# An LSTM with residual on one core: the input product x·Wx by blocks of 4 steps, replaced by blocks of 24 steps with 20 outer and 7 inner products of 256 columns

## The chip, the core and the metric

The kernel runs on one core of a Trainium2 chip. The metric is the time on the device in microseconds (us), from one launch. Before the change, three runs took 3149.18, 3149.30 and 3149.34 us, so the median is 3149.3 us. The trace comes from one profiled execution.

## The reference, cut to what matters

The input `x` has 32 sequences of 512 steps of 512 values. An LSTM with 512 units runs over the 512 steps, from the state `cond_1024`, and its hidden states are added to `x`. Everything is in float32.

```python
xW = jnp.einsum('ntd,dg->ntg', x, Wx) + b        # all steps: 512 x 2048 weights
def step(carry, xw_t):
    prev_h, prev_c = carry
    a = xw_t + prev_h @ Wh                        # 32 x 512 times 512 x 2048
    i, f, o = sigmoid(a[:, :H]), sigmoid(a[:, H:2*H]), sigmoid(a[:, 2*H:3*H])
    g = jnp.tanh(a[:, 3*H:])
    next_c = f * prev_c + i * g
    next_h = o * jnp.tanh(next_c)
    return (next_h, next_c), next_h
x = x + swapaxes(hs, 0, 1)
```

The recurrent product `prev_h @ Wh` can only be made step by step. The input product `x Wx` is known for all steps from the start, so a kernel is free to make it in any order and by any bilinear scheme.

## The kernel before, in words

**Layout.** A step's 32 sequences are 32 columns of the stationary operand. Four such matmuls, one per quarter `j` of the gates' columns, write to the four 32-row quarters of one PSUM bank and run side by side in the array, so that the gates of a step fill a bank of 128 x 512 numbers.

**A step.** `h_part` (L584) makes the recurrent product: 16 matmuls of 512 columns for one step, accumulated on a bank that already holds the step's input part and bias. `cell` (L614 to L651) is the chain that leads to the next step: three activations on ScalarE, the products `fc`, `ig` and the sum `c` on VectorE, the tanh of `c` (L630), the product `h` (L633) and two 32x32 block transposes to `ht` (L642), on which the next `h_part` waits. GpSimd adds `x` to `ht` for the output (L648), and SyncE stores two steps at a time (L651).

**The input part.** While the chain of `cell` runs, TensorE has to be given other work: the input product of later steps. It is made for four steps at a time (a "quad") by two nested schemes of 7 products in place of 8: `operand` and `inner` (L380) make 7 x 7 products of 4 matmuls with 128 columns each. The sums of weights that the scheme needs lie in SBUF for the whole run (`w_sb`, made at the start by L253 and L258), the sums of `x` are made on VectorE per 8 steps (`early_sums`, `late_sums`, L127 to L171), and the products are put together on VectorE and ScalarE from PSUM (`read_out`, `first_add`, `second_add`, `seed`, L313 to L372, L510 to L519) straight into the banks of the gates. Nothing of it leaves the core.

**Order.** The program order is written by hand: a loop over windows `k` (one per step, after a head) emits `h_part`, the evacuations, the sums of `x`, the input products (`input_part`) and `cell`, and each engine runs its own instructions in that order. The recurrent product of step `t` comes before the input products of the window on TensorE's queue, and `cell` comes behind the evacuations and the sums on VectorE's and ScalarE's queues. The first quads and the last four steps are made with plain products (`direct`, L411).

Of the kernel before, what the change touches and what calls it, by code (L numbers as in the profile page):

```python
# [9 lines left out]
PSUM = bass.MemoryType.PSUM  # L10

# [5 lines left out]
TC = 8  # L17
NCHUNK = T // TC

FIRST = 2  # L20
LAST = T // 4 - 1

SPLIT = 4 * LAST - 2

LEAD = 11
BEGIN = {1: 0, 5: 1, 6: 3, 7: 6, 2: 7, 3: 7, 4: 9}
WINDOWS = T + LEAD

TAIL = T - 19

H = P // 2
# [3 lines left out]
def kernel(  # L35
# [8 lines left out]
):  # L44

    nc = tc.nc

    const = ctx.enter_context(tc.tile_pool(name="const", bufs=1))
    xpool = ctx.enter_context(tc.tile_pool(name="xpool", bufs=3))  # L80
    spool = ctx.enter_context(tc.tile_pool(name="spool", bufs=2))
    upool = ctx.enter_context(tc.tile_pool(name="upool", bufs=1))
    opool = ctx.enter_context(tc.tile_pool(name="opool", bufs=2))
    work = ctx.enter_context(tc.tile_pool(name="work", bufs=1))
    psum = ctx.enter_context(tc.tile_pool(name="psum", bufs=1, space=PSUM))


    pa = [psum.tile([P, 4, P], F32, name=f"pa_{i}") for i in range(3)]
    slot = {1: (0, 0), 7: (0, 1), 5: (1, 0), 4: (1, 1), 6: (2, 0), 2: (2, 1), 3: (2, 2)}
    pb = psum.tile([P, 4, P], F32, name="pb")  # L90
    pbslot = {1: 0, 7: 0, 5: 0, 4: 1, 6: 0, 2: 1, 3: 2}
    pp = psum.tile([P, 4, P], F32, name="pp")
    ge = psum.tile([P, G, P], F32, name="ge")
    go = [psum.tile([P, G, P], F32, name=f"go_{i}") for i in range(2)]

    split_banks = [(ge, pp), (go[1], ge), (pa[1], pa[0]), (pa[2], pb), (go[0], pp), (ge, go[1])]

    def is_split(t):
        return t == 0 or t >= SPLIT

    def bank_of(t, h):

        return (ge, pa[2])[h] if t == 0 else split_banks[t - SPLIT][h]

    def half_of(t, h):

        return bank_of(t, h)[:, 0:2]

    def gates_of(t):
        return ge if t % 2 == 0 else go[(t % 4) // 2]  # L110


    xcs, sums = {}, {}

    def load_chunk(c):
        xc = xpool.tile([P, TC, NJ, B], F32, name=f"xc_{c}", tag="xc")
        nc.sync.dma_start(out=xc.rearrange("p t q b -> p (t q b)"), in_=x[c])
        xcs[c] = xc

    def blocks(c):  # L120

        return xcs[c].rearrange("p (d r s) (k e) b -> p d r s k e b", d=2, r=2, s=2, k=2, e=2)

    def pair_sums(eng, dst, a11, a12, a21, a22):

        return [
            lambda: eng.tensor_add(dst[0], a21, a22),  # L127
            lambda: eng.tensor_sub(dst[1], dst[0], a11),
            lambda: eng.tensor_sub(dst[2], a11, a21),
            lambda: eng.tensor_sub(dst[3], a12, dst[1]),  # L130
        ]

    def inner_sums(eng, dst, a11, a12, a21, a22):
        return pair_sums(eng, [dst[:, i] for i in range(4)], a11, a12, a21, a22)

    def early_sums(eng, c, ds=(0, 1)):

        if c not in sums:
            s = spool.tile([P, 2, 2, 2, 2, B], F32, name=f"sa_{c}", tag="sa")
            n = spool.tile([P, 4, 4, B], F32, name=f"na_{c}", tag="na")  # L140
            n1 = spool.tile([P, 4, 2, B], F32, name=f"n1_{c}", tag="n1")
            sums[c] = {"sa": s, "na": n, "n1": n1}
        v, s, n, n1 = blocks(c), sums[c]["sa"], sums[c]["na"], sums[c]["n1"]
        z = s.rearrange("p i d s e b -> p (i d) s e b")
        if len(ds) == 1:
            d = slice(ds[0], ds[0] + 1)
            v, s, n1 = v[:, d], s[:, :, d], n1[:, :, d]
            n, z = n[:, :, ds[0] :: 2], z[:, ds[0] :: 2]
        f = s.rearrange("p i d s e b -> p i d s (e b)")
        w = v.rearrange("p d r s k e b -> p d r s k (e b)")  # L150
        return [
            *inner_sums(eng, n1, *(v[:, :, 0, i, 0, e] for i in range(2) for e in range(2))),
            lambda: eng.tensor_add(f[:, 0], w[:, :, 1, :, 0], w[:, :, 1, :, 1]),
            lambda: eng.tensor_sub(f[:, 1], f[:, 0], w[:, :, 0, :, 0]),
            *inner_sums(eng, n, *(z[:, :, i, e] for i in range(2) for e in range(2))),
        ]

    def late_sums(eng, c):

        v = blocks(c)  # L160
        s = spool.tile([P, 2, 2, 2, 2, B], F32, name=f"sb_{c}", tag="sb")
        n = spool.tile([P, 4, 4, B], F32, name=f"nb_{c}", tag="nb")
        n2 = spool.tile([P, 4, 2, 2, B], F32, name=f"n2_{c}", tag="n2")
        sums[c] |= {"sb": s, "nb": n, "n2": n2}
        f = s.rearrange("p i d s e b -> p i d s (e b)")
        fa = sums[c]["sa"].rearrange("p i d s e b -> p i d s (e b)")
        w = v.rearrange("p d r s k e b -> p d r s k (e b)")
        z = s.rearrange("p i d s e b -> p (i d) s e b")
        return [
            lambda: eng.tensor_sub(f[:, 0], w[:, :, 0, :, 0], w[:, :, 1, :, 0]),  # L170
            lambda: eng.tensor_sub(f[:, 1], w[:, :, 0, :, 1], fa[:, 1]),  # L171
            *inner_sums(eng, n, *(z[:, :, i, e] for i in range(2) for e in range(2))),
            *inner_sums(eng, n2, *(v[:, :, :, i, 1, e] for i in range(2) for e in range(2))),
        ]

    INNER = {1: (0, 0), 2: (0, 1), 4: (1, 1)}
    SUM = {5: 0, 6: 1, 7: 2, 3: 3}

    def operand(r, s, quad):

        c, d = divmod(quad, 2)
        z = sums[c]
        if r in INNER:
            big, k = INNER[r]
            if s in INNER:
                i, e = INNER[s]
                return blocks(c)[:, d, big, i, k, e]
            return z["n1"][:, SUM[s], d] if r == 1 else z["n2"][:, SUM[s], d, big]
        group = "a" if r in (5, 6) else "b"
        i = {5: 0, 6: 1, 7: 0, 3: 1}[r]  # L190
        if s in INNER:
            return z["s" + group][:, i, d, INNER[s][0], INNER[s][1]]
        return z["n" + group][:, SUM[s], 2 * i + d]

    bias_sb = const.tile([P, G, P], F32, name="bias_sb")
    h_init = const.tile([P, NJ, B], F32, name="h_init")
    w_sb = {r: const.tile([P, 8 if r == 1 else 7, NJ, P], F32, name=f"w_{r}") for r in range(1, 8)}
    w12 = const.tile([P, 4, NJ, P], F32, name="w12")  # L200
    raw = {(0, 0): w_sb[1], (0, 1): w12, (1, 0): w_sb[2], (1, 1): w_sb[3]}

    wh_sb = const.tile([P, NJ - 1, NJ, G * P], F32, name="wh_sb")
    wh_3 = const.tile([P, 2, NJ, G * H], F32, name="wh_3")

    def wh_of(k, j, i=None):

        halves = slice(0, 2) if i is None else slice(i, i + 1)
        if k == NJ - 1:
            return wh_3[:, halves, j]  # L210
        return wh_sb[:, k, j].rearrange("p (i c) -> p i c", i=2)[:, halves]

    def load_raw(k, gg):
        nc.sync.dma_start(
            out=raw[k, gg][:, 0:4].rearrange("p s j u -> p (s j u)"),
            in_=wx[2 * k + gg],
        )

    def load_steps(a, b, c=0):

        if c not in xcs:
            xcs[c] = xpool.tile([P, TC, NJ, B], F32, name=f"xc_{c}", tag="xc")
        nc.sync.dma_start(
            out=xcs[c][:, a:b].rearrange("p t q b -> p (t q b)"),
            in_=x[c][:, a * P : b * P],
        )


    bias_t = const.tile([P, G * NJ], F32, name="bias_t")
# [3 lines left out]
    load_steps(0, 4)  # L233
    load_raw(0, 0)
    load_raw(0, 1)
    load_steps(0, 4, 1)
    load_raw(1, 0)
    load_raw(1, 1)
    load_steps(4, 5)
    nc.sync.dma_start(out=h_init.rearrange("p q b -> p (q b)"), in_=h0)  # L240
    for k in range(NJ - 1):
        nc.sync.dma_start(out=wh_sb[:, k].rearrange("p j c -> p (j c)"), in_=wh[:, k])
    for i in range(2):
        nc.sync.dma_start(
            out=wh_3[:, i].rearrange("p j c -> p (j c)"),
            in_=wh[:, NJ - 1, i * NJ * G * H : (i + 1) * NJ * G * H],
        )
    load_steps(4, 8, 1)
    load_steps(5, 8)

    def outer_weight(r):
# [71 lines left out]
    def slot_of(r, quad):  # L323

        if r == 6 and quad == FIRST:
            return (1, 2)
# [546 lines left out]
```

## Time and profile before

| | |
|---|---|
| median of 3 runs | 3149.3 us |
| span of the profiled execution | 3147.8 us (the median run is 1.5 us longer than it) |
| TensorE busy | 3140.9 us, 100% of the span, granted clock 1.000 |
| VectorE busy | 2263.4 us, 72% |
| ScalarE busy | 1288.8 us, 41% |
| GpSimd busy | 232.8 us, 7% |
| moved by DMA | 86.23 MB, mean 27 GB/s |

The page of the profile gives the busy time of each engine (PE is TensorE's matmuls, DVE is VectorE, ACT is ScalarE, POOL is GpSimd, SP is SyncE). The timeline gives instructions in order of time: start, duration, engine, line, operation, output and inputs, shape, and how many were merged into the row. A float32 matmul stands as two instructions, so that "x8" is four matmuls. Starts of back-to-back rows show the pace of an engine better than durations, since instructions are pipelined and overlap.

### The profile page before, as it was taken

What the parts mean: (1) busy time and instruction counts of PE and PEld (TensorE: products, weight loads), DVE (VectorE), ACT (ScalarE), POOL (GpSimd) and SP (SyncE); (2) the same over time, 40 slices, a digit from 0 to 9 for tenths busy, and PEclk for the clock granted to TensorE, in tenths of its full rate; (3) what the DMA queues carried; (4) which work ended last, traced back from release to release, by engine and by line L of the source; (5) the groups of instructions that cost most, each with busy time, mean ns of one, the idle gap of its engine ahead of it and who ended that gap; (6) DMA issues with size and microseconds to landing.
All of it is one profiled execution on the core that took longest, in us unless ns stands there. A gap on an engine that the chain in (4) does not pass through costs nothing.

```text
span 3147.8 us, 150115 instructions
## 1 busy us (share of the span) xinstructions
PE 3140.9 (100%) x66384; PEld 1901.1 (60%) x66384; DVE 2263.4 (72%) x9338; ACT 1288.8 (41%) x4274; POOL 232.8 (7%) x505
## 2 busy tenths in 40 slices
PE   9999999999999999999999999999999999999999
PEld 5666666666666666666666666666666666666665
DVE  8777777777777777777777777777777777777775
ACT  3444444444444444444344444444344444444343
POOL 1000000000000000000000000000000000000000
PEclk9999999999999999999999999999999999999999
DMA  3000000000000000000000000000000000000000
GB/s 137 26 26 21 26 28 20 28 20 27 27 20 28 20 28 26 21 26 20 28 26 21 26 27 21 28 20 26 28 20 28 20 28 27 21 27 20 28 20 29
DMA packets 49325, 86.23 MB, mean 27 GB/s; under 512 B 5792, under 2 KB 38944, under 8 KB 47776
## 3 DMA queue, kind: packets, MB, share of 16 engines
q1 hardware_dynamic: 48528, 76.63, 7.6%
q8 instruction: 518, 8.49, 1.1%
q14 instruction: 135, 1.11, 0.1%
q10 hardware_dynamic: 144, 0.01, 0.0%
HBM read 43.07 MB, written 33.55 MB: 24 GB/s over the span
## 4 chain that ended last, share of the span: by engine, by line
PE 100%; DMA 0%; DVE 0%; ACT 0%; issue 0%; SPq 0%
PE go L584 28%; PE ge L584 28%; PE pa L380 18%; PE pp L380 10%; PE pb L380 6%; PE ge L380 5%; PE go L380 3%; PE go L411 1%; PE pa L584 0%; PE pp L411 0%; PE pa L411 0%; DMA w<-in_L_cond_Wx_dram 0%; PE pa L438 0%; PE pp L584 0%; PE ge L411 0%; PE ge L438 0%
## 5 line engine op out<-in xcount | busy, mean ns | idle before, releaser
L584 PE MATMUL go<-wh_sb,ht 128*32 128x512 f32 (+1 forms) x6144 | 702.8, 590 | 0.0
L584 PE MATMUL ge<-wh_sb,ht 128*32 128x512 f32 (+1 forms) x6120 | 700.0, 590 | 0.0
L618 DVE TENSOR_TENSOR fc<-s,c 128x128 f32<-128x128 f32 x489 | 143.0, 292 | 496.1 <-ACT s L614 496.1
L614 ACT ACTIVATE s<-ge 128x256 f32<-128x256 f32 (+1 forms) x263 | 99.5, 378 | 829.1 <-PE ge L584 825.5
L648 POOL TENSOR_TENSOR oc<-xc,ht 128x128 f32<-128x128 f32 x493 | 228.1, 463 | 2806.6 <-issue 1404.0
L584 PEld LDWEIGHTS ge<-wh_sb,ht 128*32 128x32 f32 x6120 | 192.8, 110 | 304.8 <-issue 264.4
L584 PEld LDWEIGHTS go<-wh_sb,ht 128*32 128x32 f32 x6144 | 190.9, 110 | 307.0 <-issue 301.3
L380 PE MATMUL pa<-w,n 128*32 128x128 f32 x6000 | 301.1, 273 | 0.0
L630 ACT ACTIVATE ig<-c 128x64 f32<-128x64 f32 x1024 | 208.4, 248 | 222.5 <-DVE c L628 208.8
L614 ACT ACTIVATE s<-go 128x256 f32<-128x256 f32 (+1 forms) x265 | 100.0, 377 | 431.8 <-PE go L584 431.8
L584 PE MATMUL go<-wh,ht 128*32 128x512 f32 (+1 forms) x2048 | 265.2, 590 | 0.0
L584 PE MATMUL ge<-wh,ht 128*32 128x512 f32 (+1 forms) x2040 | 264.2, 590 | 0.0
L633 DVE TENSOR_TENSOR fc<-s,ig 128x64 f32<-128x64 f32 x1024 | 191.0, 225 | 96.0 <-ACT ig L630 96.0
L380 PEld LDWEIGHTS pa<-w,n 128*32 128x32 f32 x6000 | 182.0, 110 | 77.5 <-issue 39.5
L380 PEld LDWEIGHTS pa<-w,na 128*32 128x32 f32 x4000 | 124.6, 110 | 149.5 <-issue 109.9
L318 ACT COPY u<-pp 128x512 f32<-128x512 f32 x250 | 146.6, 586 | 142.4 <-PE pp L380 142.3
L380 PE MATMUL pa<-w,na 128*32 128x128 f32 x4000 | 200.7, 273 | 0.0
L380 PE MATMUL pp<-w,sa 128*32 128x128 f32 x4000 | 200.7, 273 | 0.0
L380 PE MATMUL pa<-w,nb 128*32 128x128 f32 x4000 | 200.7, 273 | 0.0
L642 DVE STREAM_TRANSPOSE ht<-fc 128x64 f32<-128x64 f32 x978 | 182.2, 224 | 1.5 <-DVE fc L633 1.0
L623 DVE TENSOR_TENSOR ig<-s 128x64 f32<-128x64 f32 x1024 | 183.1, 218 | 0.0
L628 DVE TENSOR_TENSOR c<-fc,ig 128x64 f32<-128x64 f32 x978 | 172.9, 218 | 0.0
(195 smaller groups left out, 5686.5 us busy)
## 6 DMA issues: line engine op xcount, KB each, us to landing
out_dram<-oc SPq DMA_DIRECT2D x255, 128.0 KB, 1.8
xc<-in_x_dram SPq DMA_DIRECT2D x62, 512.0 KB, 3.9
w<-in_L_cond_Wx_dram SPq DMA_DIRECT2D x4, 1024.0 KB, 8.6
wh_sb<-in_L_cond_Wh_dram SPq DMA_DIRECT2D x3, 1024.0 KB, 15.2
wh<-in_L_cond_Wh_dram SPq DMA_DIRECT2D x2, 512.0 KB, 15.0
w<-in_L_cond_Wx_dram SPq DMA_DIRECT2D x2, 512.0 KB, 5.2
xc<-in_x_dram SPq DMA_DIRECT2D x3, 256.0 KB, 7.7
xc<-in_x_dram SPq DMA_DIRECT2D x1, 192.0 KB, 11.4
```

The lines of the kernel that those rows point to most:

```text
L318: nc.scalar.copy(u, pp)
L380: nc.tensor.matmul(dst[j * B : (j + 1) * B], operand(r, s, quad), w_sb[r][:, place(r, s), j], start=start, stop=True, skip_group_check=True,)
L411: nc.tensor.matmul(half_of(t, gg)[j * B : (j + 1) * B] if is_split(t) else bank[j * B : (j + 1) * B, 2 * gg : 2 * gg + 2], xcs[c][:, tt, 2 ...
L584: nc.tensor.matmul(g[j * B : (j + 1) * B], state["ht"][:, k, :], wh_of(k, j, i), start=False, stop=True, skip_group_check=True,)
L614: nc.scalar.activation(s[:, i, 0:2], g[:, :, 0:2], AF.Sigmoid)
L618: nc.vector.tensor_mul(by_half(fc), s[:, :, 1], by_half(state["c"]))
L623: nc.vector.tensor_mul(ig[:, u], s[:, i, 0], s[:, i, 3])
L628: nc.vector.tensor_add(c[:, HALVES[i]], fc[:, HALVES[i]], ig[:, HALVES[i]])
L630: nc.scalar.activation(tc_t[:, HALVES[i]], c[:, HALVES[i]], AF.Tanh)
L633: nc.vector.tensor_mul(h[:, u], s[:, i, 2], tc_t[:, u])
L642: nc.vector.transpose(ht[:, 2 * i : 2 * i + 2].rearrange("p q b -> p (q b)"), h[:, HALVES[i]])
L648: (nc.gpsimd if t < TAIL else nc.vector).tensor_add(state["oc"][:, tt % 2], xcs[n][:, tt], ht)
```

## The change

The input product of steps 32 to 511 is made in 20 blocks of 24 steps (3 rows of 8 steps). Each block is a bilinear scheme of 20 outer products over 3x2 by 2x4 blocks, given as tables (`A_OPS`: 13 sums of x blocks, `B_OF`: which blocks of Wx are summed per product, `C_OPS`: 25 sums of products, `C_OF`: the 12 results). Each outer product is made by 7 inner products of 4 matmuls with 256 columns. One outer product is begun per window, five in six windows (`begin`).

- **Weights.** 14 of the 20 products need a sum of blocks of Wx. These sums are made on VectorE in the steps 0 to 9 (`make_factors`), stored to DRAM (`kept`) and loaded again for every block of 24 steps (`fetch`: 384 KB and 512 KB per product).
- **x.** The 13 sums of x blocks (`node_sums`) and four inner sums per product (`inner_sums`) are made on VectorE, in `prepare`, emitted behind `cell` of the window before.
- **Products.** `evacuate` copies and adds the inner products (ScalarE L297, L301, L307, L308; VectorE L304, L309), and `finish_product` makes the sums of `C_OPS` on VectorE, in halves of 512 columns, in 7 SBUF slots.
- **Results.** A finished result, 8 steps by a quarter of the gates, is written to DRAM in four DMAs, so that it lies by step (`store`). Per step, `load_xw` loads 256 KB back three steps ahead, GpSimd adds the bias (`add_bias`, L418, 128 x 512), and ScalarE copies the sum into the bank of the gates (`seed_gates`, L437).
- **Head and tail.** Steps 0 to 7 are plain products (`direct`), steps 8 to 31 are 12 units of 2 x 7 inner products (`finish_unit`). The last product ends in step 494 or before; from step 495 on a step is split into two halves of the units.
- `h_part` and `cell` are as before in their instructions, but the split form is used only in the tail.

The diff is nearly the whole kernel; its core is the new functions:

```diff
+    def make_factors(n):
+        wa, wb = ring(n, f"make_{n}")
+        (first, s0), *rest = B_OF[n]
...
+    def inner_sums(a, name):
+        s = spool.tile([P, 4, 4, B], F32, name=f"s_{name}", tag="sums")
...
+            lambda: v.tensor_add(s[:, 0], a(1, 0), a(1, 1)),
+            lambda: v.tensor_sub(s[:, 1], s[:, 0], a(0, 0)),
+            lambda: v.tensor_sub(s[:, 2], a(0, 0), a(1, 0)),
+            lambda: v.tensor_sub(s[:, 3], a(0, 1), s[:, 1]),
...
+    def products(v):
+        for late, ss in ((1, (6,)), (4, (4,)), (2, (7,)), (0, (1,)), (0, (5,)), (1, (5,)), (3, (2, 3))):
+            job = jobs.get(v - late)
+            for s in ss if job else ():
+                if s != 5 or job.w5 == v:
+                    product(job, s)
...
+    def evacuate(v):
+        for half, late in ((1, 5), (0, 4)):
+            job = jobs.get(v - late)
+            if job:
+                job.finish(half)
...
+        job = jobs.get(v - 2)
+        if job:
+            nc.vector.tensor_add(job.pu[:, 1], job.acc, job.p5)
+        job = jobs.get(v - 3)
+        if job:
+            nc.scalar.copy(job.pp[0], job.pu)
+            nc.scalar.copy(job.pp[1][:, 0], job.acc)
+            nc.vector.tensor_add(job.pp[1][:, 1], job.acc, job.p5)
...
+        def finish(half):
+            pp = job.pp[half].rearrange("p n c -> p (n c)")
+            if n in copied:
+                nc.scalar.copy(slot(n, half), pp)
...
+            for v in by_ready[n]:
+                how, a, b = C_OPS[v - R]
+                fn = nc.vector.tensor_add if how == "add" else nc.vector.tensor_sub
+                srcs = source(a), source(b)
+                fn(slot(v, half), *srcs)
...
+    def load_xw(t):
+        xw[t] = upool.tile([P, 2, C], F32, name=f"xw_{t}", tag="xw", bufs=4)
+        i, a = divmod(t, ROW)
+        nc.sync.dma_start(out=xw[t].rearrange("p n c -> p (n c)"), in_=stored[i][a])
+
+    def add_bias(t):
+        nc.gpsimd.tensor_add(xw[t], xw[t], bias_sb)
...
+        for k in range(T):
+            if k % 2 == 0 and k + 2 < T:
+                load_residual(k + 2)
+            if 2 * 4 - 3 <= k and k + 3 < T:
+                load_xw(k + 3)
+            h_part(k)
+            if 1 <= k < T - 1:
+                seed_gates(k + 1)
+            if 2 * 4 - 2 <= k and k + 2 < T:
+                add_bias(k + 2)
+            for m, v in enumerate(windows_of(k)):
...
+                evacuate(v)
+                products(v)
+                fetch(v)
...
+                if m == 0:
+                    cell(k)
+                    for _ in range(make_at.get(k, 1 if k < START else 0)):
+                        if to_make:
+                            for op in make_factors(to_make.pop(0)):
+                                op()
+                for op in prepare(v + 1):
+                    op()
+                if m == 0 and k < 3:
+                    direct(k + 5, gates[k % 2])
+                    keep_direct(k + 5, gates[k % 2])
```

More of the change, by code (lines that the diff above doesn't have):

```diff
@@ L214, in load_raw, with load_row @@
+    raw = [const.tile([P, 4, C], F32, name=f"raw_{i}") for i in range(8)]
+    tt_ = [const.tile([P, 4, C], F32, name=f"t_{i}") for i in range(8)]
+    single = {b[0][0] for b in B_OF if len(b) == 1}
+    rows, xw, stored = {}, {}, {}
+    def load_row(i, a=0, b=ROW):
+        if i not in rows:
+            rows[i] = xpool.tile([P, ROW, NJ, B], F32, name=f"row_{i}", tag="row")
         nc.sync.dma_start(
-            out=raw[k, gg][:, 0:4].rearrange("p s j u -> p (s j u)"),
-            in_=wx[2 * k + gg],
-        )
@@ new lines, with store @@
+    free = []
+    spare = [const.tile([P, 2, 2 * C], F32, name=f"slot_{i}") for i in range(3)]
+    free += spare
+    others = [t for i in range(8) if i not in single for t in (raw[i], tt_[i])]
+    def store(i, j, f):
+        if i not in stored:
+            stored[i] = dram.tile([ROW, P, 2 * C], F32, name=f"xw_{i}", tag="xw", bufs=6)
+        to = stored[i].rearrange("(g t) p c -> t p g c", g=2)
+        for t in range(4):
+            nc.sync.dma_start(out=to[t, j * B : (j + 1) * B], in_=f[t * B : (t + 1) * B])
@@ new lines, in finish_unit @@
+    def finish_unit(job, i, j):
+        def finish(half):
+            if half == 0:
+                job.f = free.pop(0)
+            nc.scalar.copy(job.f[:, half], job.pp[half].rearrange("p n c -> p (n c)"))
+            if half:
+                store(i, j, job.f)
+                free.append(job.f)
+        return finish
+    ready = list(range(R))
+    for _, a, b in C_OPS:
+        ready.append(max(ready[a], ready[b]))
+    by_ready = {n: [R + i for i in range(len(C_OPS)) if ready[R + i] == n] for n in range(R)}
@@ L743 @@
+    to_make = [n for n in range(R) if len(B_OF[n]) > 1]
+    make_at = {0: 2, 1: 2, 2: 2, 3: 2}
     with tc.manual_schedule():
@@ new lines @@
+        for m in range(10):
+            nc.tensor.matmul(
+                pps[0][0:B].rearrange("p n c -> p (n c)"),
+                c_init[:, 0:B],
+                c_init.unsqueeze(1).to_broadcast([P, 4, P]),
+                start=True,
+                stop=True,
+            )
+        nc.vector.transpose(
+            bias_sb.rearrange("p n (m l) -> p (n m) l", l=B),
+            bias_t.unsqueeze(2).to_broadcast([P, G * NJ, B]),
+        )
+        firsts = [gates[0], gates[1], pps[0], pps[1]]
```

885 lines of the change are left out of this document (327 added, 558 removed).

## The prediction

> **What bounds the kernel now.** I read the page first (busy time and the chain that ended last), then two stretches of windows, then the timeline of one step.
>
> ```profile
> span 3147.8 us, 150115 instructions
> PE 3140.9 (100%) x66384; PEld 1901.1 (60%) x66384; DVE 2263.4 (72%) x9338; ACT 1288.8 (41%) x4274; POOL 232.8 (7%) x505
> ...
> PE 100%; DMA 0%; DVE 0%; ACT 0%; issue 0%; SPq 0%
> ```
>
> ```profile
> 600.00:746.88 146.88, 146.88 (x3136) 89.25 (x3132) 105.44 (x438) 60.46 (x199) 11.03 (x24) 1.00 0.08 24
> ...
> 6.00:16.20 10.20, 9.59 (x188) 7.17 (x192) 8.95 (x21) 0.60 (x2) 0.00 (x0) 1.00 1.00 388
> ```
>
> TensorE never stops, at a granted clock of 1.00; 24 steps take 146.88 us, in which VectorE is busy 105.44. One step, from its first recurrent matmul to the next one:
>
> ```profile
> 1500.62 2.76 PE L584 MATMUL go<-wh_sb,ht 128*32 128x512 f32 x24
> ...
> 1504.06 0.40 PE L380 MATMUL pa<-w,nb 128*32 128x128 f32 x8
> ...
> 1504.31 0.39 ACT L614 ACTIVATE s<-go 128x256 f32<-128x256 f32 x1 [1.33 <-PE go L584]
> ...
> 1504.72 0.29 DVE L618 TENSOR_TENSOR fc<-s,c 128x128 f32<-128x128 f32 x1 [1.28 <-ACT s L614]
> ...
> 1506.07 0.37 DVE L642 STREAM_TRANSPOSE ht<-fc 128x64 f32<-128x64 f32 x2
> ...
> 1506.52 0.46 POOL L648 TENSOR_TENSOR oc<-xc,ht 128x128 f32<-128x128 f32 x1 [5.76 <-DVE ht L642]
> ...
> 1506.68 2.76 PE L584 MATMUL ge<-wh_sb,ht 128*32 128x512 f32 x24
> ```
>
> The recurrent product takes 1504.06 - 1500.62 = 3.44 us. The 12 input products behind it take 2.62 us, so 0.218 each. Beside them runs the chain: `fc` starts 0.66 us after the recurrent product, the transposes end at 1506.44, which is 1.72 after `fc`. The next recurrent matmuls need only the first half of `ht`, some 0.15 earlier; with 0.06 for the hand-over they could start 1.63 after `fc`, so 2.29 us after the recurrent product. That the input products last longer than 2.29 us is what hides the chain. This is the number to watch.
>
> **The change part by part.**
>
> *TensorE, gain.* The new products have 256 columns. Products of that width stand at the start:
>
> ```profile
> 6.61 1.07 PE L411 MATMUL go<-w,xc 128*32 128x256 f32 x16 [1.43 <-DMA w<-in_L_cond_Wx_dram]
> 7.47 1.07 PE L411 MATMUL ge<-w,xc 128*32 128x256 f32 x16
> ```
>
> Two groups of four in 0.86-0.865, so 0.4315 us per product. A block of 24 steps has 20 x 7 = 140 products: 60.4 us, and 24 x 3.44 = 82.6 of recurrent product, 143.0 together against 146.88. All of TensorE's work: 512 x 3.44 = 1761.3; 20 x 60.4 = 1208.2; 12 units x 14 x 0.4315 = 72.5; 8 plain steps of 3.44 = 27.5; in all 3069.5. With the same start at 6.6 and the 4.5 us from the last recurrent matmul (row below, 3142.80 + 0.43 to 3147.8), the time without any stall would be 3080.6, 67 us less than now. The rest of the sum is stalls.
>
> *Tail, loss 21.9 us.* The last products thin out: the steps 490 to 494 have 4, 3, 1, 0 and 0 products against the 2.29 us that the chain needs: stalls of 0.56, 1.0, 1.86, 2.29 and 2.29, together 8.0. From 495 on there are none, but a step is split in halves. The pace of split steps stands at the end of the trace:
>
> ```profile
> 3135.40 1.05 PE L584 MATMUL go<-wh_sb,ht 128*32 128x256 f32 x16
> ...
> 3137.59 1.05 PE L584 MATMUL pp<-wh_sb,ht 128*32 128x256 f32 x16
> ...
> 3139.42 0.24 DVE L635 STREAM_TRANSPOSE ht<-fc 128x64 f32<-128x64 f32 x1
> ...
> 3142.80 0.61 PE L584 MATMUL go<-wh,ht 128*32 128x256 f32 x8
> ```
>
> The first half is ready 2.19 us into a step (from 3135.40 to 3137.59), its transpose ends at 3139.66; with 0.05 the next step starts after 4.31, 0.87 more than its work. 16 times 0.87 is 13.9.
>
> *Head, loss 18.5 us.* VectorE makes the weight sums here, and its queue is in order.
>
> ```profile
> L513 DVE TENSOR_TENSOR p<-u,p 128x512 f32<-128x512 f32 x125 | 86.5, 692 | 114.7 <-ACT u L318 114.7
> L372 DVE TENSOR_TENSOR go<-pa,u 128x512 f32<-128x512 f32 x125 | 85.9, 687 | 0.0
> ...
> L253 DVE TENSOR_TENSOR w<-w,w 128x2048 f32<-128x2048 f32 x4 | 9.1, 2285 | 0.5 <-DMA w<-in_L_cond_Wx_dram 0.5
> ```
>
> From 512 to 2048 columns 1.04 ns each, so 768 columns take 0.95. An addition of `make_factors` (256 and 768 columns) is then some 1.3 to 1.37 us and the four closing ones 1.43. In step 0 VectorE has, behind the chain (2.4 after the recurrent product), two sets of factors with 1 and 3 additions (8.2), the sums for the next unit (2.7), a 512-column and a 256-column addition (1.0): 14.3. TensorE needs the last of them for inner product 7 of unit 0, after 2.6 + 3.44 + 0.86 = 6.9. It waits 7.4. The same sum gives 1.9 in step 1, 3.3 ahead of step 0 (unit 0's sums come behind the keep of step 4) and 5.9 in the steps 2 to 12. By the Trainium skill, TensorE: Matmul & The Clock Gate, section "What's actually happening", an idle window of about 3.4 us halves TensorE's clock until it has been busy for as long again. An estimate by that page is some 2 us more at step 0; no idle time of that length behind the start is in this trace, whose clock is 1.00 throughout.
>
> So without the steady part: 3080.6 + 21.9 + 18.5 = 3121.
>
> *Steady part: VectorE's queue.* VectorE's evacuations and sums of x stand on its queue ahead of `fc` of the next step, and it is on VectorE that the change adds: 13 x-block sums, 80 inner sums, 50 halves of C_OPS, 40 additions of 256 columns per 24 steps.
>
> ```profile
> 1506.54 0.41 DVE L342 TENSOR_TENSOR xr<-pb,bias_sb 128x256 f32<-128x256 f32 x1
> ...
> 1506.87 0.41 DVE L367 TENSOR_TENSOR u<-pa,u 128x256 f32<-128x256 f32 x1
> ```
>
> ```profile
> 3100.16 0.69 DVE L372 TENSOR_TENSOR go<-pa,u 128x512 f32<-128x512 f32 x1
> 3100.76 0.42 DVE L486 TENSOR_TENSOR pa<-pa,bias_sb 128x256 f32<-128x256 f32 x1
> ```
>
> ```profile
> 42.92 0.46 POOL L648 TENSOR_TENSOR oc<-xc,ht 128x128 f32<-128x128 f32 x1 [5.80 <-DVE ht L635]
> 43.34 1.28 POOL L258 TENSOR_TENSOR w<-w 128x512 f32<-128x512 f32 x1
> ```
>
> ```profile
> 43.47 0.42 DVE L356 TENSOR_TENSOR pp<-pa,u 128x256 f32<-128x256 f32 x1
> 43.80 0.97 DVE L127 TENSOR_TENSOR n<-xc 128x128 f32<-128x128 f32 x1
> 44.80 0.29 DVE L128 TENSOR_TENSOR n<-n,xc 128x128 f32<-128x128 f32 x1
> 45.01 0.28 DVE L129 TENSOR_TENSOR n<-xc 128x128 f32<-128x128 f32 x1
> 45.22 0.29 DVE L130 TENSOR_TENSOR n<-xc,n 128x128 f32<-128x128 f32 x1
> 45.42 0.69 DVE L258 TENSOR_TENSOR w<-w 128x512 f32<-128x512 f32 x1
> ```
>
> Start to start: 256 columns 0.33, 512 columns 0.60 (0.72 where the next reads its result), four inner sums 0.94 (0.32 for the dependent one, then 0.2 each). The price per window: an x-block sum 0.72, inner sums 0.94, each C_OPS half 0.6 or 0.72, `pu` and `pp` 0.33 each. The budget: with six products (2.59) the transposes end 0.21 before the next recurrent matmuls start, and VectorE begins its next op some 0.07 earlier, as ops overlap at their ends; `fc` is due 3.44 + 0.66 = 4.10 after. So 4.38 us of other work fit, 4.68 before TensorE stalls (six products last 2.59, 0.30 more than 2.29). After a window that stalled, the transposes end later against the matmuls and the bounds are 4.08 and 4.38. Every sixth window has five products, 2.16 us, and stalls 0.13 in any case.
>
> By the tables, window 0 of a block has one x-block sum, four inner sums, four C_OPS halves, `pu` and `pp`: 0.72 + 0.94 + 2.5 + 0.66 = 4.8, or 5.0 with ScalarE's copy between (L308 waits for the C_OPS, L309 for L308); window 7 has 4.5, 18 4.4, 23 4.0, all others under 3.8. That alone stalls 0.4 in window 0 and 4 x 0.13: 0.93 per block, 18.6 in all.
>
> *What comes on top: GpSimd.* It gets a 128 x 512 addition per step (L418), right behind the addition for the output, at the time when VectorE begins with the sums of x. The rows above show what that does: the 128-column sum L127, 0.29 elsewhere, took 0.97 because it came while GpSimd's 128 x 512 op ran (43.34 to 44.62), and ended 0.15 behind it; L356, which reads PSUM, was not touched (0.42). So a VectorE op with both inputs in SBUF is held until the GpSimd op is over. In the changed kernel GpSimd runs from 0.15 to about 1.9 us after VectorE becomes free. The inner sums and x-block sums fall into this time: where they would be over after 0.94, they are over after some 2.2, 1.1 to 1.3 us later; in windows without sums, a C_OPS of two SBUF sums is held for 1.0. With the full hold, VectorE's work in windows 0 to 23 is 6.1, 4.2, 3.7, 4.0, 3.0, 1.4, 4.7, 5.7, 3.8, 3.4, 4.9, 3.7, 4.8, 4.7, 3.7, 4.6, 4.9, 3.7, 5.5, 4.9, 4.4, 4.2, 4.9, 5.0. Against the bounds, the stalls are 1.8 (window 0), 1.36 (7), 0.90 (18), 0.65 (23), 0.49 (15, 20), 0.44 (19), five of 0.19 to 0.25, and the rest: 7.7 per block, 154 in all. With three quarters of the hold the same sum gives 4.2 and 84, with half 2.4 and 48, with a quarter 1.4 and 28. The lower bound is no hold (18.6), as VectorE might get ahead between two GpSimd ops; the upper one the full hold. The nearest row is the full one, but a single row with one long op does not show who goes first when both wait. I take the middle between three quarters and full: 119.
>
> *Hidden.* The bias is added and loaded two to three steps ahead. ScalarE has at most 2.9 us of copies per window against some 4.3. The weights come two windows ahead of their use. Per block DMA moves 12.5 MB of weights, 6.3 out and 6.3 back of results, 4.7 of x and output: 30 MB in some 148 us, 200 GB/s, where the second row of windows has 388 GB/s at a DMA share of 1.00. That is cover of nearly two; the DMA issues stay hidden behind it.
>
> Sum: 3121 + 119 = 3240 of span, 1.5 more as a median: **3242 us**, 2.9% slower.
>
> **The rivals.**
>
> - *VectorE is not held* (the other side). If VectorE's sums go ahead of GpSimd's addition, or the addition comes later, while VectorE works on PSUM: 3121 + 18.6 + 1.5 = 3141, 0.26% faster. For it: nothing in the trace shows the two waiting for one another again and again. Against: the one row that has the pair. The point where it decides is a quarter of the hold, 28 us, where the time is 3150.
> - *Half the hold*: 3121 + 48 + 1.5 = 3171.
> - *DMA becomes the bound.* 200 GB/s is eight times the present 24; all issues are on one queue (SP), in order, where loads stand behind stores that wait for VectorE. If only half of the 388 GB/s came through, 194, a block would take 155 us in place of 148.9 (143.0 + 5.9): with the rest as above 3242 + 20 x 6 = 3360. For it: the 388 GB/s were reached with 8 KB per partition and DMA, and most of the new ones have 2 to 4 KB. Against: the weights have two windows of time, and the issues are few (some six per window).
>
> **How the numbers follow.** Three quarters to full hold, or a little beside it (3185 to 3300): 0.64. Half or a third of it (3156 to 3185): 0.08. A quarter (3143 to 3156): 0.06. None (below 3143): 0.14. DMA-bound (above 3300): 0.08. The range 3135 to 3300 takes in the bounds of the hold and most of the fast side. 0.2% (6 us) is about what a measurement of this kernel can tell from no change. Faster 0.14, within 0.2% 0.06, slower 0.80.
>
> **What would show it.** Right: 24 steps take about 149 us (143.9 if VectorE is not held), TensorE idle some 6 us of them, `fc` (L486) released late by VectorE's own queue and not by ScalarE; inner sums (L203 to L206) that take 0.9 to 1.2 us where they meet L418; the longest stall in the window of four C_OPS halves and an x-block sum; TensorE idle 7 us in step 0; a pace of 4.3 us in the tail. Wrong: inner sums of 0.29 throughout and 24 steps in 144 us, or TensorE waiting for `wa`, `wb` or `xw` from DMA.

## The result, and the profile after

The changed kernel takes **3448.6 us** (median of 4 runs, 3446.5 to 3450.5) against 3149.3 us: 1.095 times as long, interval 1.093 to 1.097. The forecast had the sign, but at 3242 us and with a range up to 3300 it missed by 207 us. The result lies above 3300 us, where the forecast had put only a bound by DMA, with 0.08; the runs below show another cause.

The page of the changed kernel, first the busy time per engine, then the engines of the chain that ended last:

```profile
span 3444.4 us, 103490 instructions
PE 3170.1 (92%) x40948; PEld 1295.2 (38%) x40948; DVE 2858.1 (83%) x8502; ACT 1529.9 (44%) x4972; POOL 960.3 (28%) x1003
...
DVE 45%; PE 37%; ACT 6%; issue 6%; DMA 5%; POOL 1%; SPq 1%; DVEq 0%; POOLq 0%; ACTq 0%
```

TensorE, 100% before, now stands still 8% of a longer span, and VectorE carries the largest part of the chain, where it had 0%. The span divides by the starts of the recurrent matmuls: step 10 begins at 178.8 us (before: 89.6), the 480 steps of the blocks end at 3323.3, the last 22 steps take 121.1 us (before: 126.4). A block of 24 steps takes 157.2 us on the mean of 20, against 146.6 before over the same steps and 143.0 without a stall. One block in the view of windows (length, then busy time of PE, PEld, DVE, ACT, POOL, then granted clock, DMA share and GB/s):

```profile
1750.27:1907.95 157.68, 146.62 (x1892) 59.27 (x1888) 134.35 (x399) 71.93 (x232) 45.60 (x49) 1.00 0.63 193
```

One window of the block, the eighth, in the timeline, from one recurrent product to the next:

```profile
1480.58 3.64 PE L452 MATMUL gates<-wh_sb,ht 128*32 128x512 f32 x32
...
1481.26 0.83 DVE L236 TENSOR_TENSOR n<-n,n 128x512 f32<-128x512 f32 x1
...
1481.50 1.72 POOL L418 TENSOR_TENSOR xw<-xw,bias_sb 128x512 f32<-128x512 f32 x1
1482.12 1.25 DVE L203 TENSOR_TENSOR s<-n 128x128 f32<-128x128 f32 x1
1483.41 0.29 DVE L204 TENSOR_TENSOR s<-s,n 128x128 f32<-128x128 f32 x1
...
1484.03 0.68 DVE L380 TENSOR_TENSOR t<-pp,raw 128x512 f32<-128x512 f32 x1
...
1485.35 0.42 DVE L309 TENSOR_TENSOR pp<-acc,p 128x256 f32<-128x256 f32 x1
1485.68 0.28 DVE L486 TENSOR_TENSOR fc<-s,c 128x128 f32<-128x128 f32 x1
...
1485.83 0.64 PE L273 MATMUL acc<-wa,s 128*32 128x256 f32 x8 [1.61 <-DVE pp L309]
...
1488.44 3.62 PE L452 MATMUL gates<-wh_sb,ht 128*32 128x512 f32 x32
```

Two things are to be seen. L203, 0.29 us where it meets nobody, takes 1.25 and ends just behind GpSimd's L418, which itself takes 1.72 in place of 1.33 because it waited for L236: each holds the other. And TensorE, done with the recurrent product at 1484.02, starts its first inner product only at 1485.83, behind L309. That is 1.81 us, and the window lasts 7.86 us, 1.83 more than 3.44 + 6 x 0.4315 = 6.03. `fc` was due at 1484.68 and came at 1485.68, 1.00 late, but this is hidden: the products that came late outlast the chain.

The view of waits shows that this is the rule (us in all, times, longest):

```profile
PE acc L273 <- DVE pp L309: 180.4, 184, 3.9
PE acc L273 <- DVE pu L304: 47.6, 43, 8.1
PE gates L452 <- DVE fc L490: 15.3, 8, 2.8
PE gates L452 <- DVE ht L507: 5.7, 5, 2.2
```

`acc` are the accumulators in PSUM; VectorE reads them in L304, which writes `pu`, and in L309, which writes `pp`. TensorE waits 228 us at the inner products for VectorE's reads of the accumulators, and 5.7 us for `ht`, the end of the chain that the forecast had watched.

### The profile page after: what moved, and what is told of

Same layout as the page of the kernel before. It is cut to its first block, busy times and chain, and to the rows that moved or that the text cites. A ratio compares the mean times of both kernels' runs of the same rounds, so it can differ in the third digit from the quotient of the medians.

```text
span 3444.4 us, 103490 instructions
## 1 busy us (share of the span) xinstructions
PE 3170.1 (92%) x40948; PEld 1295.2 (38%) x40948; DVE 2858.1 (83%) x8502; ACT 1529.9 (44%) x4972; POOL 960.3 (28%) x1003
## 4 chain that ended last, share of the span: by engine, by line
DVE 45%; PE 37%; ACT 6%; issue 6%; DMA 5%; POOL 1%; SPq 1%; DVEq 0%; POOLq 0%; ACTq 0%
PE gates L452 20%; PE acc L273 7%; DVE s L204 7%; PE pp L273 7%; DVE slot L380 4%; DVE n L236 4%; DMA row<-in_x_dram 4%; DVE s L203 3%; DVE pp L309 3%; DVE ht L507 3%; DVE s L205 3%; DVE raw L380 3%; DVE t L380 2%; DVE fc L498 2%; DVE ig L491 2%
## 5 line engine op out<-in xcount | busy, mean ns | idle before, releaser
L452 PE MATMUL gates<-wh_sb,ht 128*32 128x512 f32 (+1 forms) x16320 | 1820.0, 587 | 21.0 <-DVE fc L490 15.3
L513 POOL TENSOR_TENSOR oc<-xr,ht 128x128 f32<-128x128 f32 x495 | 304.2, 615 | 2406.6 <-DVE ht L507 1196.0
L452 PEld LDWEIGHTS gates<-wh_sb,ht 128*32 128x32 f32 x16320 | 521.6, 110 | 1033.0 <-issue 819.2
L418 POOL TENSOR_TENSOR xw<-xw,bias_sb 128x512 f32<-128x512 f32 x504 | 675.6, 1341 | 63.3 <-DMA xw<-xw 54.6
L482 ACT ACTIVATE s<-gates 128x256 f32<-128x256 f32 (+1 forms) x511 | 195.3, 382 | 695.0 <-PE gates L452 694.4
L307 ACT COPY pp<-pu 128x512 f32<-128x512 f32 x412 | 246.1, 597 | 368.6 <-DVE slot L380 166.8
L273 PE MATMUL acc<-wa,s 128*32 128x256 f32 x2240 | 176.5, 387 | 160.3 <-DVE pp L309 157.7
L204 DVE TENSOR_TENSOR s<-s,n 128x128 f32<-128x128 f32 x280 | 288.4, 1030 | 9.7
L308 ACT COPY pp<-acc 128x256 f32<-128x256 f32 x412 | 146.9, 357 | 332.6 <-DVE slot L380 126.1
L437 ACT COPY gates<-xw 128x512 f32<-128x512 f32 x493 | 284.8, 578 | 20.0 <-DVE xw L410 19.7
L309 DVE TENSOR_TENSOR pp<-acc,p 128x256 f32<-128x256 f32 x412 | 175.5, 426 | 89.5 <-ACT pp L308 80.5
L273 PE MATMUL pp<-wb,n 128*32 128x256 f32 x3200 | 245.9, 379 | 0.0
L491 DVE TENSOR_TENSOR ig<-s 128x64 f32<-128x64 f32 x1024 | 187.3, 223 | 0.0
L297 ACT COPY pu<-acc 128x256 f32<-128x256 f32 x412 | 152.4, 370 | 50.7 <-PE acc L273 41.5
```

Of the source, the lines that this page charges most:

```text
L204: lambda: v.tensor_sub(s[:, 1], s[:, 0], a(0, 0)),
L273: nc.tensor.matmul(dst[t * B : (t + 1) * B], a[:, t], w, start=s in (1, 5) and m == 0, stop=True, skip_group_check=True,)
L307: nc.scalar.copy(job.pp[0], job.pu)
L309: nc.vector.tensor_add(job.pp[1][:, 1], job.acc, job.p5)
L418: nc.gpsimd.tensor_add(xw[t], xw[t], bias_sb)
L437: nc.scalar.copy(gates[t % 2], xw[t])
```

## The experiments

Three explanations stood beside one another: the bias addition of GpSimd that holds VectorE (**hold**); the wait of the first inner product, 6, for L309 (**bank**: a job is one outer product on its way through the windows, and product 6 of one job adds to an accumulator that lies in one PSUM bank with the accumulator, two jobs older, that L309 reads); and the 190 GB/s of DMA.

**The hold and the order, alone and together.**

```diff
-            if 2 * 4 - 2 <= k and k + 2 < T:
-                add_bias(k + 2)
```

> The bias addition of GpSimd (L418) is left out from step 8 on, so those gates lack their bias; nothing else changes. Theory (GpSimd's bias addition holds VectorE's additions with two SBUF inputs, and the first inner product of the next window, 6, waits for VectorE's last evacuation L309 because both use one PSUM bank, so every microsecond by which VectorE is late is one of idle TensorE): VectorE gets about 1.1 us back per window, the inner sums fall from 1.03 us to 0.29, the block of 24 steps goes from 157.2 us to about 145, the tail loses about 12 us of its 121, the total is 3185 to 3200 us. Rival 1 (the DMA traffic of 190 GB/s bounds the window): the block stays at 157, total about 3440. Rival 2 (VectorE's work is too much with or without the hold): the sums shorten, but the block stays above 153, total 3360 or more.

```diff
-        for late, ss in ((1, (6,)), (4, (4,)), (2, (7,)), (0, (1,)), (0, (5,)), (1, (5,)), (3, (2, 3))):
+        for late, ss in ((4, (4,)), (0, (5,)), (1, (5,)), (3, (2, 3)), (2, (7,)), (0, (1,)), (1, (6,))):
```

> Only the order of TensorE's seven inner products within a window changes: 6, 7 and 1 (which need an accumulator bank that VectorE has just read, or sums that it has just made) go last, 4, 5, 3 and 2 first; the whole computation stays. Theory (wait of product 6 for L309 on the same PSUM bank, 10.7 us per block): that wait goes, the lateness of VectorE for fc (6.1 us per block) stays, so the block goes from 157.2 us to about 149 and the total to about 3280 us. Rival 1 (the prediction's step: only fc is late, the wait ahead of the products merely moves the same lateness): the block stays at 155 to 158, total 3400 to 3450. Rival 2 (DMA bound): unchanged.

> The bias addition of GpSimd is left out from step 8 on as in e1_no_bias, and the products are ordered as in e2_order. Theory: neither cause is left, the block is 143.5 to 144.5 us (143.0 without any stall), the total about 3160 us. If the hold alone carried the loss, this would equal e1_no_bias within 5 us; if the bank alone did, it would equal e2_order but for the tail (about 15 us).

Measured: without the bias 3248.7 us, block 148.0; with the other order 3293.8, block 150.2; both 3202.0, block 146.2. The eleventh block in the windows of the three kernels, in this order:

```profile
1660.46:1808.14 147.68, 145.13 (x1893) 59.90 (x1888) 112.20 (x399) 71.69 (x232) 14.55 (x25) 1.00 0.65 206
```

```profile
1670.15:1819.90 149.75, 146.03 (x1892) 59.42 (x1884) 132.38 (x399) 70.65 (x233) 45.80 (x48) 1.00 0.66 204
```

```profile
1626.92:1771.86 144.94, 143.94 (x1893) 60.74 (x1888) 112.05 (x399) 72.11 (x232) 14.71 (x25) 1.00 0.66 209
```

DMA as the bound falls: it moves the same blocks in less time, at 204 to 209 GB/s. VectorE is busy 134.35 us in a block with the hold and 112.20 without: 22 us per block are waiting inside its instructions. The two causes stand in for each other. Each alone brings most of the gain (9.2 and 7.0 us per block), together 11.0 and not 16.2, since a VectorE that is not late has nothing to pass on, and a lateness that is not passed on at the first product has slack up to `fc`. In the kernel with the other order, the eighth window of a block is this:

```profile
1714.36 3.64 PE L452 MATMUL gates<-wh_sb,ht 128*32 128x512 f32 x32
...
1715.91 1.25 DVE L203 TENSOR_TENSOR s<-n 128x128 f32<-128x128 f32 x1
...
1717.82 0.61 PE L273 MATMUL pp<-wb,n 128*32 128x256 f32 x8
...
1719.13 0.43 DVE L309 TENSOR_TENSOR pp<-acc,p 128x256 f32<-128x256 f32 x1
1719.47 0.28 DVE L486 TENSOR_TENSOR fc<-s,c 128x128 f32<-128x128 f32 x1
...
1721.11 1.48 PE L452 MATMUL gates<-wh_sb,ht 128*32 128x512 f32 x10 [0.52 <-DVE ht L507]
```

VectorE is held as before (1.25), the products start at once, `fc` is 1.01 late (due at 1718.46), and the window lasts 6.75: a stall of 0.72, which is 1.01 less the 0.30 of slack of a window with six products.

All three are slower than the theory's number: by 49 us without the bias, by 14 with the order, by 42 with both. What was missed shows in the kernel with both edits, where all windows of a block but one take 5.75 to 6.05 us, and the first takes 8.4 (median of 20). Its view of waits has the row:

```profile
DVE n L236 <- DMA row<-in_x_dram: 40.3, 20, 4.8
```

Once per block VectorE waits for a row of x, because the first node sum needs the first and the third row and the third is asked for last.

**The bias on VectorE, then the rows in another order.** The first of these two kernels keeps the other order of products, the next adds the row order to that:

```diff
-        nc.gpsimd.tensor_add(xw[t], xw[t], bias_sb)
+        nc.vector.tensor_add(xw[t], xw[t], bias_sb)
```

> The order of products of e2_order, and the bias is added by VectorE in place of GpSimd; the whole computation stays. Theory: VectorE gains a 128x512 addition (estimate 0.6 us, from L309's 128x256 at 0.35 and the 1.0 us held sums that go away) per window, but is no longer held, so the block is 144 to 146 us and the total 3175 to 3215 us. Rival (VectorE's load alone, 2858 us busy before any addition, is the bound): the block is 150 or more, total above 3290 us.

```diff
-            load_row(HEAD // ROW + MO * sb + rest)
+            load_row(HEAD // ROW + MO * sb + (0, 2, 1)[rest])
```

> e4_dve with one more edit: a block's three rows of x are loaded in the order first, third, second. In e3_both and e4_dve one window of each block is left over, the one at the block's border: 8.42 and 8.74 us against 6.02, and in it VectorE's first node sum (L236, first row plus third row) waits up to 4.8 us for the row's DMA. Theory (the third row is asked for one window before it is needed): that window falls to 6.1 to 6.6 us, the block from 147.3 us to about 145, the total from 3225 to about 3175 us. Rival (the four combinations of 128x512 that fall in that window make VectorE late without any DMA, as the prediction had it): the window stays above 7.5 us, total above 3200.

Measured: 3224.8 us with a block of 147.6, 10 us above what was expected; then 3199.9 (interval of the ratio to before 1.014 to 1.018) with 146.1. So it is cheaper to give VectorE 0.68 us more work per step than to have it held. The row order took off 25 us and the wait for the row is gone, but 50 were expected: the first window still takes 7.4 us, with `fc` 1.6 late. Theory and rival have about half of it each; what else is late there is VectorE's own work of that window.

**Shorter pieces on GpSimd.** With the order of products and of rows:

```diff
-        nc.gpsimd.tensor_add(xw[t], xw[t], bias_sb)
+        for n in range(2):
+            for c in range(0, C, P):
+                u = slice(c, c + P)
+                nc.gpsimd.tensor_add(xw[t][:, n, u], xw[t][:, n, u], bias_sb[:, n, u])
```

> The order of products of e2_order and the row order of e5_rows; the bias stays on GpSimd, but in four additions of 128x128 in place of one of 128x512. Theory A (the hold lasts as long as one GpSimd instruction, so VectorE gets in between the pieces): VectorE's inner sums fall from 1.0 us to at most 0.6, the block goes to 144 to 146 us, total about 3180 us. Theory B (the pieces take the port back each time, or their longer sum holds as much): block 149 to 151 less the 2 us of the row order, total 3240 or more, the tail of 120 us as long as in e2_order.

Measured: 3198.1 us, block 145.7, tail 116.2. Groups of the changed kernel (busy us, mean ns, then idle time ahead), and of this one:

```profile
L204 DVE TENSOR_TENSOR s<-s,n 128x128 f32<-128x128 f32 x280 | 288.4, 1030 | 9.7
...
L205 DVE TENSOR_TENSOR s<-n 128x128 f32<-128x128 f32 x280 | 121.5, 434 | 0.0
...
L206 DVE TENSOR_TENSOR s<-n,s 128x128 f32<-128x128 f32 x280 | 78.1, 279 | 0.0
```

```profile
L206 DVE TENSOR_TENSOR s<-n,s 128x128 f32<-128x128 f32 x280 | 147.0, 525 | 0.0
L205 DVE TENSOR_TENSOR s<-n 128x128 f32<-128x128 f32 x280 | 146.2, 522 | 0.0
...
L204 DVE TENSOR_TENSOR s<-s,n 128x128 f32<-128x128 f32 x280 | 120.7, 431 | 9.7
```

The dependent inner sum takes 431 ns in place of 1030 (322 where GpSimd adds no bias at all), but the two sums behind it are now held too: 522 and 525 ns in place of 434 and 279. Over the blocks VectorE is busy 123.4 us per block, against 132.3 with the same order of products and the addition in one piece, and 111.8 without it. So the pieces take off some two fifths of the hold, not all of it. The steady part is still better than with the bias on VectorE, although GpSimd is longer busy. Theory A holds for the blocks. Its total is 18 us too low, 8 of them in the tail, which GpSimd's pieces still disturb (108.1 with the bias on VectorE).

**The bank, and product 6 alone.** Both keep the bias on GpSimd.

```diff
-        job.acc = accs[w % 2][:, w // 2 % 2]
+        job.acc = accs[w // 2 % 2][:, w % 2]
```

> The changed kernel with one edit: the accumulators of jobs 2m and 2m+1 lie in one PSUM bank, in place of those of 2m and 2m+2; the order of the products, the bias on GpSimd and all else stay. Theory (product 6 of job v-1 waits for VectorE's L309 on job v-3 only because both accumulators lie in one bank): now it shares a bank with job v-3 in no window, so the wait for L309 ahead of the first product (10.7 us per block, 9.1 of it in odd windows) goes; in odd windows product 7 meets it 0.86 us later and keeps about 2.4 us per block, in even windows L304, 0.4 us ahead of L309, keeps about 1. The block falls from 157.2 us to 149.5 to 152, the total to about 3290 to 3345 us. Rival (the bank plays no part; TensorE waits for data of VectorE's queue): block 157, total about 3440 us.

```diff
-        for late, ss in ((1, (6,)), (4, (4,)), (2, (7,)), (0, (1,)), (0, (5,)), (1, (5,)), (3, (2, 3))):
+        for late, ss in ((4, (4,)), (2, (7,)), (0, (1,)), (0, (5,)), (1, (5,)), (3, (2, 3)), (1, (6,))):
```

> The changed kernel with product 6 alone moved from first to last place in a window; the bias stays on GpSimd. Theory as corrected by e7_bank (the lateness of VectorE's queue stays, and comes out at the next product that shares a bank with what VectorE reads): product 7, now second, waits for L304 of its own job, and product 1 behind it too, 0.86 us later than product 6 waited for L309 at the head, so 2.5 to 6 us of the 10.7 per block are left, the block is 150 to 154 us, the total 3290 to 3380 us. Rival 1 (product 6 alone is the cause, 7 and 1 play no part): as e2_order, block 149.9, total 3294 us or less. Rival 2 (its place plays no part): 157 and 3448 us.

In the first of the two, product 1 of a pair's second job starts the bank in which the first job still accumulates, so that the sums of every second job are changed; its instructions are those of the changed kernel. By the Trainium skill, PSUM — Partial Sum Buffer, section "PSUM: the matmul accumulator", such a start makes the next addition of the other group overwrite; no row here shows it. Measured: 3389.9 us, block 154.3, which is outside of what was expected. Then 3336.8 us, block 151.9, within it. The waits of TensorE at the products, first of the other banks, then of product 6 moved:

```profile
PE acc L273 <- DVE pu L304: 119.5, 164, 9.0
PE acc L273 <- DVE pp L309: 41.7, 57, 4.7
```

```profile
PE acc L273 <- DVE pu L304: 107.2, 146, 9.0
```

The place of the accumulators does decide which instruction TensorE waits for: L309 had 180.4 us and has 41.7, or nothing. But much of it comes back at the next product whose bank VectorE still reads (L304: 47.6 before, now 119.5 and 107.2): of the 7.0 us per block that the full order wins, the first edit wins 2.9 and the second 5.3. The first expectation took each window by itself. As these waits suggest, VectorE's queue is late by the hold in any case, and TensorE meets it somewhat further on, in each window again. The order with products 7 and 1 near the end as well wins the other 1.7 us. An accumulator tile is one bank in all these kernels, so the runs do not tell a wait for the bank from a wait for the tile.

**The hold where VectorE has slack**, in the kernel before:

```diff
                 h_part(t)
+                for _ in range(4 if 4 <= t < TAIL else 0):
+                    nc.gpsimd.tensor_sub(h_init, h_init, h_init)
```

> The kernel before, with four idle subtractions of 128x128 per step added on GpSimd in the stretch in which the changed kernel adds the bias (from step 4 to the tail; they compute zeros that nothing reads). Theory (the hold as such costs nothing where VectorE has slack: before, VectorE is busy 72% and waits about 1.0 us per step for the sigmoid ahead of fc): VectorE's additions with two SBUF inputs that meet them get up to 0.5 us longer, the time grows by under 1%, to 3150 to 3180 us. Rival (whatever holds VectorE costs as much as in the changed kernel, some 0.4 us per step): 3300 us or more.

Measured: 3149.4 us against 3149.5, ratio 1.000 (0.999 to 1.001). In the groups, before and with the four operations:

```profile
L618 DVE TENSOR_TENSOR fc<-s,c 128x128 f32<-128x128 f32 x489 | 143.0, 292 | 496.1 <-ACT s L614 496.1
...
L127 DVE TENSOR_TENSOR n<-xc 128x128 f32<-128x128 f32 (+1 forms) x127 | 32.5, 256 | 0.0
```

```profile
L618 DVE TENSOR_TENSOR fc<-s,c 128x128 f32<-128x128 f32 x489 | 143.1, 293 | 429.8 <-ACT s L614 429.8
...
L127 DVE TENSOR_TENSOR n<-xc 128x128 f32<-128x128 f32 (+1 forms) x127 | 55.5, 437 | 0.0
```

VectorE is held here too (L127 takes 437 ns in place of 256), and the 66 us come out of the time in which `fc` waited for ScalarE anyway (496.1 - 429.8). The price is nothing: a hold of this size costs nothing in a queue that has slack. It is a smaller hold than the changed kernel's, though. VectorE is busy 66 us longer in all (2329.4 against 2263.4), 0.13 us per step, where the changed kernel loses 0.92 (22 us in 24 steps). Whether the 1.0 us of slack per step would take that as well was not tried.

**The tail.**

```diff
-        nc.gpsimd.tensor_add(xw[t], xw[t], bias_sb)
+        (nc.vector if is_split(t) else nc.gpsimd).tensor_add(xw[t], xw[t], bias_sb)
```

> The changed kernel, with the bias added by VectorE in place of GpSimd for the split steps of the tail alone. Theory (two bias additions of GpSimd back to back hold fc and ig of every second split step): all split steps pass at about 4.4 us, the stretch from step 490 to the end falls from 121.1 us to about 108.5, as in the kernels without GpSimd's additions (109.1, 109.3, 108.4), and the total from 3448.6 to about 3436 us; the blocks stay at 157.2. Rival (the tail is late because xw comes back late from DRAM): unchanged, 121 us and 3448.

Measured: 3436.6 us, within a microsecond of what was expected; the last 22 steps take 108.1 us in place of 121.1, the blocks stay at 157.3. The timeline of two split steps of the changed kernel:

```profile
3384.87 3.66 PE L452 MATMUL pp<-wh_sb,ht 128*32 128x256 f32 x64 [0.73 <-DVE fc L490]
3386.95 2.51 POOL L418 TENSOR_TENSOR xw<-xw,bias_sb 128x512 f32<-128x512 f32 x2 [8.77 <-DMA xw<-xw]
3387.60 0.72 DVE L490 TENSOR_TENSOR fc<-s,c 128x64 f32<-128x64 f32 x1 [1.23 <-ACT s L482]
3388.24 1.30 DVE L491 TENSOR_TENSOR ig<-s 128x64 f32<-128x64 f32 x1
...
3390.84 3.66 PE L452 MATMUL gates<-wh_sb,ht 128*32 128x256 f32 x64 [2.31 <-DVE fc L490]
```

The data of two steps come together, GpSimd adds twice, and two products of the chain, 0.2 us each, take 0.72 and 1.30: this step lasts 5.97 us, its neighbours 4.39.

**All that helped, together.** The order of products and rows, the pieces, VectorE in the split steps, and

```diff
-    make_at = {0: 2, 1: 2, 2: 2, 3: 2}
+    make_at = {0: 0, 1: 2, 2: 3, 3: 2, 4: 2}
```

> What helped, together: the order of products, the row order, GpSimd's bias in pieces of 128x128 but on VectorE in the split steps, and the sums of weights made in steps 1 to 9 and none in step 0. Theory: blocks of 145.7 us as in e6_pieces, the tail 108.4 in place of 116.2 us, step 0 at 19 to 21 us in place of 24.6 (the first is 8 us, the second 4 to 5 us less than e6_pieces with 3198 us): 3180 to 3190 us, still over the 3149.5 of the kernel before, since its first ten steps end at 165 us against 89.6 there and 20 blocks at 145.7 in place of 146.6 win back under 25 us. Rival (the sums of weights have to be early, or the tail of e6_pieces is long for another reason): 3195 us or more.

Measured: 3187.2 us (ratio 1.0122, interval 1.0105 to 1.0139). The chain is again TensorE's:

```profile
span 3186.6 us, 105469 instructions
...
PE 70%; DVE 18%; issue 5%; DMA 3%; ACT 2%; POOL 1%; SPq 1%; DVEq 0%; POOLq 0%; ACTq 0%
```

It is 261 us faster than the changed kernel and still slower than the one before. Against that one, step 10 begins 70.4 us later (160.0 against 89.6), 20 blocks at 145.85 win 14.7, and the last 22 steps win 16.9 (109.5 against 126.4): +38.8 of span. Had its blocks no stall at all, at 143.0, it would be some 18 us ahead (70.4 - 71.8 - 16.9). So most of what the scheme can win is spent on its head.

## Why the prediction was wrong, point by point

- **TensorE's work: right.** 143.0 us per block was forecast without stalls; the windows without a stall show it, in the kernel with both edits (6.02 us against 6.03 with six products, 5.75 against 5.60 + 0.13 with five).
- **The hold: right as a mechanism,** read from a single row with L127 and L258 of the kernel before. VectorE's instructions take 22 us per block longer by it.
- **The step that failed: "`fc` is due 3.44 + 0.66 = 4.10 after. So 4.38 us of other work fit".** This counted VectorE's queue against one deadline. There is an earlier one: product 6, first on TensorE, must not write a bank that L309 reads, so L309, which stands just ahead of `fc`, is due at 3.44. By the forecast's own terms 3.44 + 0.21 + 0.07 = 3.72 us fit ahead of that, not the 4.68 that it allowed before TensorE stalls. The forecast had a product wait for VectorE only in the head, and there for sums of weights. By the Trainium skill, PSUM — Partial Sum Buffer, section "PSUM bank collisions raise a hardware error", two engines must be kept apart by bank and not by address; that the program has such a wait agrees with the 180.4 us at L309. The stall per block is 14.2 us in place of 5.95: 165 of the 204 us of span that were missing. With the order of products changed, the forecast's sum comes out: 7.1 us per block (150.2 - 143.0), between its 4.2 for three quarters of the hold and its 7.7 for the full one, and that with the row's DMA in it.
- **The head: mis-sized by 23 us.** The forecast's own terms put step 10 at 156.1 us (3240 - 20 x 148.92 - 105.5 for the last 22 steps, each of 3.44, with 8 products, 4.5 of end and the 21.9 of stalls); it was 178.8. Against the shortest that any kernel here shows for the same work (13.56 us for step 0, 18.9 for 1 and 2, 9.48 for each of 3 to 7, and 9.0 for step 9), TensorE loses 9.1, 4.9, 4.6, 5.5, 1.9 and 3.6 us in the steps 0, 1, 2, 4, 7 and 9, 29.6 in place of 15.2. The order of products again: with it changed these losses are 13.0, though step 0 begins 3.5 us later. Some 8 us are left. Of these, 3.7 are the start: the first product with weights begins at 10.30, behind the ten warm-up products of L586, and not at the 6.6 that the forecast took over from the kernel before.

```profile
1.05 9.83 PE L586 MATMUL pp<-c_init 128*32 128x512 f32 x19 [1.05 <-DVE c_init L133]
...
10.30 0.63 PE L399 MATMUL gates<-raw,row 128*32 128x512 f32 x3
```

  Another 2.1 are step 9, where even the shortest, 9.0, is above its work of 3.44 + 8 x 0.4315 = 6.9. Part of the 29.6 may be the clock, which the forecast had left out of the sum:

```profile
40.00:50.00 10.00, 4.25 (x48) 1.30 (x40) 9.66 (x19) 0.37 (x1) 0.20 (x1) 0.92 0.37 143
50.00:60.00 10.00, 7.67 (x84) 3.06 (x88) 5.87 (x13) 2.10 (x5) 0.00 (x0) 0.74 0.11 43
```

  Behind the long wait of step 0 the granted clock falls to 0.92 and 0.74, and to 0.83 in four more stretches of 10 us. The busy time of all six times the missing share is 7.5 us at most. This agrees with the Trainium skill, TensorE: Matmul & The Clock Gate, "What's actually happening", where idle time of some 3.4 us throttles the clock; what it costs by itself was not tried.
- **The tail: mis-sized by 16 us.** The pace was right for every second step (4.39 against 4.31). That GpSimd's addition holds the chain itself (L490, L491) was not in the sum; taking it away gave 13.0 of the 15.6.
- **"The DMA issues stay hidden": nearly.** No bound by DMA. The wait for a row of x is 14.6 us in all in the changed kernel, and comes to the fore when the rest is faster: the row order took 1.5 us per block from the kernel with the bias on VectorE (147.6 to 146.1).
- **The rival at 3141, VectorE not held: its price was wrong as well.** Without the hold the time is 3248.7, since the head stays (step 10 at 175.4), and in the blocks window 0, the row and the bank: VectorE in time for `fc` is not yet in time for L309.

## What to carry to other kernels

For an engine's queue, list every instruction of another engine that waits for it, with the bank that they share, and take the earliest deadline, not that of the chain you know. A hold or an extra wait is priced by the slack of the queue that it hits: as many elements per step added on GpSimd cost 0 us in one kernel, in pieces that hold VectorE 0.13 us per step, and 184 (9.2 per block) in the other, where they hold it 0.92. And before the steady state is tuned, add up head and tail: here, in the best kernel, the head alone takes 70 of the 72 us that perfect blocks would win.

## What the runs showed of the hardware

- The hold between GpSimd and VectorE goes both ways and lasts to the end of the instruction that came first: VectorE's 128x128 sum 1.25 us in place of 0.29, GpSimd's 128x512 addition 1.72 in place of 1.33. In the changed kernel all 25 additions L418 that start while an L236 runs, which reads SBUF alone, take 1.72 to 1.74; the 82 that start while an addition L380 with one input from PSUM runs take 1.27 to 1.30, as do those that meet nothing. This agrees with the Trainium skill, SBUF — State Buffer, section "SBUF: two separate sides", which calls it an exclusive lock for the whole instruction.
- So the grain counts: four additions of 128x128 occupy GpSimd longer than one of 128x512 (4 x 516 ns against 1341), and hold VectorE less (the four inner sums L203 to L206 take 1887 ns together, against 2221 with one piece and 1277 without the addition).

```profile
L418 POOL TENSOR_TENSOR xw<-xw,bias_sb 128x512 f32<-128x512 f32 x504 | 675.6, 1341 | 63.3 <-DMA xw<-xw 54.6 <-ACT s L482 8.5 <-ACT pp L307 0.2
```

```profile
L421 POOL TENSOR_TENSOR xw<-xw,bias_sb 128x128 f32<-128x128 f32 x2016 | 980.8, 516 | 86.4 <-DMA xw<-xw 82.6 <-ACT pp L308 2.6 <-ACT pp L307 0.7
```
